# Attention and mixture of experts on one core: early attention, weight splits on VectorE alone, two elements routed at once, a layer norm ended on ScalarE

## The chip, the core and the metric

The kernel runs on one core of a Trainium2 chip. The core's engines run side by side, each working through its own instructions in order: TensorE (PE in the profile; its weight loads are PEld), VectorE (DVE), ScalarE (ACT), GpSimd (POOL) and SyncE (SP), which only issues transfers. They meet at semaphores. The metric is the time of one execution in microseconds of the device; the kernel before takes 1104.46 us (median of 3 runs, 1103.72 to 1105.25).

## What is computed

Four elements of 1024 tokens with 256 channels go through one layer of attention and a mixture of experts, in float32:

```python
# attention: 16 heads, head size 16, causal; queries, keys and values by a "down" and an "up" matrix
q_lat = (x @ Wq_down).reshape(b, t, H, L)        # the same for k and v
q = concat([q_lat @ Wq_up_c, rope(q_lat @ Wq_up_e)])
att = softmax(where(causal, q @ k.T / sqrt(DH), -inf))
x = layernorm(x + (att @ v) @ Wc)
# mixture of experts: 8 experts, 2 for each token
scores = (x @ router_w.T + router_b) / temp
for _ in range(3):                               # Sinkhorn, on each element by itself
    scores -= logsumexp(scores, over experts)
    scores -= logsumexp(scores, over the tokens of the element)
gates = exp(scores); gates /= sum(gates) + 1e-8
topk_gates, topk_idx = top 2 of gates, scaled to a sum of 1
out_e = (relu(x @ wg[e]) * (x @ wp[e])) @ wo[e]
x = layernorm(x + sum over the two experts of gate * out_e)
```

## The kernel before

Instructions are traced by Python in the order below; a planner then orders each engine's instructions by their readiness in a simulated time line and by priority, which is the order of tracing unless a block raises it. The order in which the engines run can thus differ from that of the source.

**Projection** (`project`, L234). For each element and half of 512 tokens, x is split into a high and a low part in a reduced 32-bit format, and products are made of three matmuls (`mm3`, L191: high x high, high x low, low x high). `split` (L186) makes the two parts: ScalarE casts the high one, and VectorE, or another engine given as `sub`, subtracts it from the source for the low one. Queries and keys are stored to DRAM as three bf16 parts; `load_stack` (L323) brings the parts of one group of four heads back as 12 transfers per call, all issued by SyncE.

**Attention** runs over *units* (L307): an element, a group of four heads, and its two halves of queries; for the last element (3) the first halves of two groups form a unit, and the second halves are four units of their own. For a unit, `row_max` (L341) computes scores (PE L354) and their maxima (DVE L360, and L363 with the causal mask), turns them and writes them into the stack of the queries. `attend` (L398) then computes transposed scores (PE L433), their exponentials (ACT L437, into one of three `pT` tiles), zeroes what lies above the diagonal (POOL L446; in the last two units DVE L442), and multiplies by the values (PE L417).

The main loop (L1086) attends the units one step (one head of one key block) after the other. In each step it traces as many steps of `row_max` as keep it 44 (`LEAD`) ahead, a share of the `lane` (projections of later elements and `finish` of the element before), and a share of the `side` lane (routing), whose budget is `SIDE` per attention step, or `SIDE3` for the last element. Every step of the routing costs at least 0.05 of it. Before the loop, the maxima of the whole first unit are traced, one step of the projection of element 1 with every third of them (L1067 to L1071).

**Finish** (`finish`, L541) of an element, in two halves: load x (`x1`, SP L548), turn and scale the attention's result, multiply by Wc (PE L588), add x (DVE L591), `layernorm` (L509: statistics on DVE L513 and L514, the reciprocal root on POOL L516 and L517, and the normal form on DVE L519), store it to two tables in DRAM (`x1_rows`, `results`), and compute the router's logits (L635).

**Routing** (`route`, L648) of an element: 3 iterations of the Sinkhorn loop and the choice of two experts, a chain of 73 small steps on DVE, ACT and PE; then 8 pairs of indirect transfers on GpSimd (L805) that write each token into the list of its expert. For elements before the last they are traced only in a window of eight attention steps of a unit (`hole`, set at L1133 from `HOLE`, L30). `lay_out` (L827) then works out which slots belong to which expert: first 17 slots that need the first three elements alone, then the others once element 3 is routed.

**Experts.** 35 slots of 256 tokens run one after the other (`slot`, L976, with `begin`, L1159, for the next slot in between). For a slot: load the three weights of its expert (SP L940, 1.5 MB), gather its tokens (POOL L926, two indirect transfers), split the weights (`halves`, L953: six pieces of 128x512, ACT L188 for the high parts and L189 for the low parts `wl`), turn and split the tokens (`rows`, L962), three-fold matmuls into `gp`, ReLU (ACT L992), product (DVE L993), split of the product (`hh` on ACT, `hl` on DVE, L188 and L189), three-fold matmuls into `eo`, scaling by the gate (ACT L1006, into one of `EO` = 6 tiles, two per slot), and two indirect transfers that add to `results` (POOL L1007). Each of them waits until those of the slot before have landed, as they may touch the same rows (L1014). One of the six pieces of `wl` is split on GpSimd, as `SH_A` and `SH_B` (L25) name it:

```python
split(a, c, d, nc.gpsimd if (i, k) in (SH_A if key < (0, NSA) else SH_B) else nc.vector)
```

At the end (L1187 on) the `results` are read back, normalised and stored.

## Time and profile before

| what | value |
|---|---|
| median of 3 runs | 1104.46 us |
| the profiled execution | 1105.71 us |
| its span, first to last instruction | 1104.0 us |
| mean granted clock of TensorE | 0.966 |
| busy in the span: PE, DVE, ACT, POOL | 983.1, 855.4, 708.0, 536.6 us |
| share of PE in the chain that ended last | 62% |
| opening and projection of element 0 | 0 to about 62 us |
| attention (first to last exponential) | 65.5 to about 699 us |
| expert slots (first turn of tokens to last matmul) | 701 to about 1066 us |
| last layer norm | 1078 to 1104 us |

A line of a window gives, for a stretch of time, the length, then for PE, PEld, DVE, ACT and POOL the busy time and in brackets the number of instructions, then the granted clock of TensorE, the share of the 16 DMA engines in use, and GB/s. Matmuls overlap each other, so PE's busy time can be full while it gets through fewer matmuls than it could; the number of instructions tells that. A line of the waits names the engine and its line that waited, then the engine and line that ended the wait, then the total in us, the number of waits and the longest. A line of a tile gives the shortest, the median and the longest duration in ns. A line of the timeline gives the start and the length in us, the engine, the line and the shapes, and in brackets the idle time of the engine before it and what ended that. A wait for several things is put down to the one that came last by the profile; where the named one had long been done, it was another, often a transfer.

The groups of small work that the change touches, as sums over the execution: layer norm's line L519 12.6 us on DVE in 32 instructions (mean 451 ns); the pair scatters L805 64.9 us on POOL in 64; GpSimd's splits of `wl` 61.2 us in 35 (mean 1750 ns); DVE's splits of `wl` 126.7 us in 175 and of `hl` 96.1 us in 140.

### The profile page before, as it was taken

To read this page: it belongs to the slowest core of one execution; us is meant where nothing else is said; L and a number is where in the kernel's file an instruction comes from. 1 tells how busy PE (TensorE), PEld (TensorE's weight loads), DVE (VectorE), ACT (ScalarE), POOL (GpSimd) and SP (SyncE) were. 2 spreads that over 40 slices of the span, in tenths; PEclk is the share of its full clock that TensorE was granted. 3 is DMA by queue.
4 is the path that set the end of the run, shared out by engine and by line. 5 is a ranking of instruction groups with operands and counts; after the bars stand their busy time and mean duration, and the time that the engine had idled before them with its cause. 6 is when DMAs were issued, how large, how long until landed. Compare 5 with 4: busy or idle time off the path is not lost.

```text
span 1104.0 us, 20951 instructions
## 1 busy us (share of the span) xinstructions
PE 983.1 (89%) x6808; PEld 621.3 (56%) x6808; DVE 855.4 (77%) x2516; ACT 708.0 (64%) x1701; POOL 536.6 (49%) x587
## 2 busy tenths in 40 slices
PE   6688999999999999999899999899995989999950
PEld 4445333355434355533344333599995989999950
DVE  4677777888987788887458885689993879898936
ACT  3345666656766666766666777677773767777733
POOL 7276511121534534431333405665778677777554
PEclk9899999999999999999999999999997999999985
DMA  8573410231331231421133210877763877898637
GB/s 297 177 227 94 130 44 16 59 102 59 115 106 30 74 96 37 143 73 35 26 101 102 50 39 3 271 221 216 216 187 110 235 212 201 221 230 223 179 41 304
DMA packets 92065, 146.33 MB, mean 133 GB/s; under 512 B 19760, under 2 KB 55088, under 8 KB 91568
## 3 DMA queue, kind: packets, MB, share of 16 engines
q1 hardware_dynamic: 69296, 108.50, 31.4%
q0 software_dynamic: 20608, 36.18, 14.2%
q8 instruction: 56, 0.92, 0.3%
q10 hardware_dynamic: 2048, 0.27, 0.2%
q14 instruction: 57, 0.47, 0.1%
HBM read 109.26 MB, written 35.38 MB: 131 GB/s over the span
## 4 chain that ended last, share of the span: by engine, by line
PE 62%; DVE 12%; ACT 8%; DMA 6%; issue 5%; POOL 4%; SPq 2%; ACTq 0%; DVEq 0%; POOLq 0%
PE y L417 13%; PE sT L433 9%; PE s L354 9%; ACT pT L437 4%; PE gp L197 4%; PE gp L195 4%; PE gp L196 4%; POOL pairs L805 3%; DVE wl L189 2%; PE po L588 2%; PE eo L195 2%; PE eo L196 2%; DVE d L363 2%; PE eo L197 2%; DMA results<-eo,ent 2%
## 5 line engine op out<-in xcount | busy, mean ns | idle before, releaser
L437 ACT ACTIVATE pT<-sT 128x512 f32<-128x512 f32 (+3 forms) x768 | 347.1, 491 | 176.9 <-PE sT L433 147.3
L363 DVE CUSTOM_DVE_ANT_0 d<-s,mask 128x128 bf16<-128x128 f32 (+3 forms) x512 | 236.8, 482 | 50.4 <-PE s L354 48.8
L433 PE MATMUL sT<-qs,ks 98*128 98x512 bf16 (+3 forms) x768 | 231.7, 328 | 15.8 <-ACT pT L437 11.1
L354 PE MATMUL s<-ks,qs 96*128 96x512 bf16 (+3 forms) x768 | 222.6, 331 | 21.3 <-DVE mx L363 8.0
L446 POOL TENSOR_SCALAR_AFFINE_SELECT pT<-pT 128x512 f32<-128x512 f32 x120 | 76.6, 639 | 278.3 <-ACT pT L437 262.1
L360 DVE TENSOR_REDUCE mx<-s 128x1 f32<-128x512 f32 x256 | 175.2, 684 | 31.4 <-PE s L354 30.1
L417 PE MATMUL y<-pT,va 128*32 128x512 f32 (+3 forms) x1536 | 183.2, 500 | 1.4 <-POOL pT L446 0.6
L197 PE MATMUL gp<-xh,wl 128*128 128x256 f32 x560 | 160.1, 287 | 17.3 <-POOL wl L189 15.3
L195 PE MATMUL gp<-xh,wh 128*128 128x256 f32 x560 | 160.7, 288 | 1.3 <-DVE relu L993 1.2
L196 PE MATMUL gp<-xl,wh 128*128 128x256 f32 x560 | 160.9, 288 | 0.0
L1007 POOL DMA_INDIRECT results<-eo,ent x70 | 113.9, 1628 | 80.7 <-issue 10.7
L354 PEld LDWEIGHTS <-qs 96*128 96x128 bf16 x768 | 71.6, 99 | 131.2 <-issue 96.7
L433 PEld LDWEIGHTS <-ks 98*128 98x128 bf16 x768 | 71.9, 99 | 123.4 <-issue 92.8
L189 DVE TENSOR_TENSOR wl<-w,wh 128x512 fp32r<-128x512 f32 x175 | 126.7, 758 | 15.1 <-ACT wh L188 14.2
L188 ACT CAST wh<-w 128x512 fp32r<-128x512 f32 x210 | 118.5, 622 | 4.9 <-DMA w<-in_wo_dram 1.6
L197 PEld LDWEIGHTS gp<-xh,wl 128*128 128x128 f32 x560 | 107.7, 193 | 18.6 <-POOL wl L189 16.4
L195 PEld LDWEIGHTS gp<-xh,wh 128*128 128x128 f32 x560 | 107.3, 192 | 2.6 <-DVE relu L993 2.4
L196 PEld LDWEIGHTS gp<-xl,wh 128*128 128x128 f32 x560 | 107.4, 192 | 0.1
L189 DVE TENSOR_TENSOR hl<-relu,hh 128x256 fp32r<-128x256 f32 x140 | 96.1, 692 | 14.1 <-ACT hh L188 12.2
L926 POOL DMA_INDIRECT xg<-x_rows,ent x70 | 81.2, 1160 | 29.5 <-issue 15.2
L188 ACT CAST hh<-relu 128x256 fp32r<-128x256 f32 x140 | 56.2, 406 | 49.8 <-DVE relu L993 49.3
L195 PE MATMUL eo<-wh,hh 128*128 128x256 f32 x280 | 80.4, 287 | 6.3 <-DVE xl L189 4.8
(208 smaller groups left out, 1702.2 us busy)
## 6 DMA issues: line engine op xcount, KB each, us to landing
w<-in_wg_dram SPq DMA_DIRECT2D x35, 512.0 KB, 5.7
w<-in_wp_dram SPq DMA_DIRECT2D x35, 512.0 KB, 4.9
w<-in_wo_dram SPq DMA_DIRECT2D x35, 512.0 KB, 4.4
ks<-parts SPq DMA_DIRECT2D x90, 128.0 KB, 2.8
qs<-parts SPq DMA_DIRECT2D x66, 128.0 KB, 2.7
parts<-lv POOLq DMA_DIRECT2D x12, 384.0 KB, 3.1
parts<-lv POOLq DMA_DIRECT2D x24, 192.0 KB, 3.1
xh<-in_x_t_dram SPq DMA_DIRECT2D x8, 512.0 KB, 3.8
```

Source lines behind the costliest of these rows:

```text
L188: nc.scalar.copy(hi, src)
L189: (sub or nc.vector).tensor_tensor(lo, src, hi.bitcast(F32), ALU.subtract)
L195: nc.tensor.matmul(ps, lhsT=sh, rhs=mh, start=(i == 0), stop=False)
L196: nc.tensor.matmul(ps, lhsT=sh, rhs=ml, start=False, stop=False)
L197: nc.tensor.matmul(ps, lhsT=sl, rhs=mh, start=False, stop=(i == n - 1))
L354: nc.tensor.matmul(ps[:, :w], lhsT=q(h, half)[:NROW, t * P : (t + 1) * P], rhs=k(h, k0 // QC)[:NROW, :w], start=True, stop=True,)
L360: nc.vector.tensor_reduce(m, ps, AX.X, ALU.max)
L363: nc.vector.tensor_tensor_reduce(out=dump[:, :w], in0=ps[:, :w], in1=mask[:, QC - w :], scale=1.0, scalar=MASKED, op0=ALU.add, op1=ALU.max ...
L417: nc.tensor.matmul(acc[g, qc][SLOT * h : SLOT * (h + 1), lo:], lhsT=va[b % 2][:, kb, at : at + SLOT], rhs=pT[:, h, lo:], start=(kb == 0), ...
L433: nc.tensor.matmul(st[:, lo:], lhsT=k(h, kb // BPQ)[: NROW + 2, kb % BPQ * P : (kb % BPQ + 1) * P], rhs=q(h, qc)[: NROW + 2, lo:], start=T ...
L437: nc.scalar.activation(pT[:, h, lo:], st[:, lo:], AF.Exp, scale=scale)
L1007: ins = nc.gpsimd.indirect_dma_start(out=results[:, :], out_offset=bass.IndirectOffsetOnAxis(ap=ent[:, j, 1:2], axis=0), in_=eo, in_offset ...
```

## The change

Six things change:

- **Splits.** `SH_A` and `SH_B` are empty, so all six pieces of `wl` of a slot are split on VectorE.
- **Begin of attention.** Before the main loop only 17 steps of `row_max` of the first unit are traced (its first half of queries), and five steps of the projection of element 1 instead of 16. The rest of the unit's maxima are traced inside the main loop, at most three steps for each attention step and never more than 44 ahead; the rest of the projection is in the lane.
- **Loads of x1.** The load of `x1` in `finish` is issued on SyncE's queue after the last transfer of a stack that was traced before it.
- **Routing.** Elements 0 and 1 are routed together, when element 1 is finished: tiles are twice as wide, the sums over tokens stay within an element, 16 pairs of scatters follow the 73 steps. Elements 2 and 3 are routed one by one as before. The pool of the routing's tiles has one buffer for each in place of two.
- **Share of the routing.** `SIDE` goes from 0.035 to 0.05 per attention step.
- **Layer norm in `finish`.** Two small instructions on GpSimd make an offset, minus mean times reciprocal root, and ScalarE applies scale and offset in place of VectorE.

```diff
@@ -15,14 +15,14 @@
-R_BUFS, X1_BUFS, PT_BUFS, SIDE, SCAT = (1,2,3,0.035,0.07)
+R_BUFS, X1_BUFS, PT_BUFS, SIDE, SCAT = (1,2,3,0.05,0.07)
-SH_A, SH_B, NSA = (((1,1),),((1,1),),0)
+SH_A, SH_B, NSA = ((),(),0)
@@ -88,7 +88,7 @@
-    sinkp = ctx.enter_context(tc.tile_pool(name="sinkp", bufs=2))
+    sinkp = ctx.enter_context(tc.tile_pool(name="sinkp", bufs=1))
@@ -515,9 +515,12 @@
         rstd = small.tile([P, BPQ], F32, tag="rstd", name=f"rstd_{n}", bufs=2)
         nc.gpsimd.tensor_scalar_add(rstd, mv[:, :, 1], EPS_LN)
         nc.gpsimd.tensor_tensor(rstd, rstd, neg_half, ALU.pow)
+        off = small.tile([P, BPQ], F32, tag="off", name=f"off_{n}", bufs=2)
+        nc.gpsimd.tensor_tensor(off, mv[:, :, 0], rstd, ALU.mult)
+        nc.gpsimd.tensor_scalar(off, off, -1.0, None, ALU.mult)
         for i in range(BPQ):
-            nc.vector.tensor_scalar(
-                x[:, i, :], x[:, i, :], mv[:, i, 0:1], rstd[:, i : i + 1], ALU.subtract, ALU.mult
+            nc.scalar.activation(
+                x[:, i, :], x[:, i, :], AF.Identity, bias=off[:, i : i + 1], scale=rstd[:, i : i + 1]
             )
 
     no_deps = {}
@@ -530,7 +533,9 @@
-    logits = {}
+    ROUTES = (*((b, b + 1) for b in range(0, B - 2, 2)), *((b,) for b in range((B - 2) // 2 * 2, B)))
+    logits, scores = {}, {}
@@ -540,14 +545,19 @@
 
     def finish(b, halves=range(NQC), alone=False):
         if b not in logits:
-            logits[b] = sinkp.tile([P, NB, E], F32, tag="lg", name=f"lg{b}")
+            bs = next(r for r in ROUTES if b in r)
+            lgs = sinkp.tile([P, len(bs), NB, E], F32, tag=f"lg{bs[0]}", name=f"lg{b}", bufs=1)
+            for j, of in enumerate(bs):
+                logits[of] = lgs[:, j]
+            scores[bs] = lgs
         lg = logits[b]
         for half in halves:
             n = f"{b}_{half}"
             x1 = work.tile([P, BPQ, C], F32, tag="x1", name=f"x1_{n}", bufs=X1_BUFS)
-            nc.sync.dma_start(
-                out=x1, in_=x_in[b, half * QC : (half + 1) * QC].rearrange("(n p) c -> p n c", p=P)
-            )
+            with tc.issue_after(queued[0].ins):
+                nc.sync.dma_start(
+                    out=x1, in_=x_in[b, half * QC : (half + 1) * QC].rearrange("(n p) c -> p n c", p=P)
+                )
             yns, zTs, pos, xTs, rts = {}, {}, {}, {}, {}
 
             def own_tile(name):
@@ -640,20 +650,26 @@
             yield 0.1
 
     def per_block(ap):
-        return ap.unsqueeze(2).to_broadcast([P, NB, E])
-
-    def per_expert(ap):
-        return ap.unsqueeze(1).to_broadcast([P, NB, E])
-
-    def route(b):
-
-        lg = logits[b]
+        return ap.unsqueeze(2).to_broadcast([*ap.shape, E])
+
+    def per_expert(ap, nb):
+        return ap.rearrange("p (b e) -> p b e", e=E).unsqueeze(2).to_broadcast([P, nb, NB, E])
+
+    def route(bs):
+
+        b, nb = bs[0], len(bs)
+        NBT, BE = nb * NB, nb * E
+        lgs = scores[bs]
+        lg = lgs.rearrange("p b n e -> p (b n) e")
 
         def tiny(name):
-            return sinkp.tile([P, NB], F32, tag=name, name=f"{name}{b}")
+            return sinkp.tile([P, NBT], F32, tag=name + str(nb), name=f"{name}{b}")
 
         def wide(name):
-            return sinkp.tile([P, NB, E], F32, tag=name, name=f"{name}{b}")
+            return sinkp.tile([P, NBT, E], F32, tag=name + str(nb), name=f"{name}{b}")
+
+        def by_element(ap):
+            return ap.rearrange("p (b n) e -> p b n e", b=nb)
 
         for it in range(SINKHORN_ITERS):
             m = tiny("sk_m")
@@ -673,44 +689,48 @@
             nc.vector.tensor_tensor(lg, lg, per_block(ls), ALU.subtract)
             yield 0.0
 
-            pm = sinkp.tile([P, E], F32, tag="sk_pm", name=f"sk_pm{b}_{it}")
-            nc.vector.tensor_reduce(pm, lg.rearrange("p n e -> p e n"), AX.X, ALU.max)
+            pm = sinkp.tile([P, BE], F32, tag=f"sk_pm{nb}", name=f"sk_pm{b}_{it}")
+            nc.vector.tensor_reduce(
+                pm.rearrange("p (b e) -> p b e", e=E), lgs.rearrange("p b n e -> p b e n"), AX.X, ALU.max
+            )
             yield 0.0
             tp = bg_tile(f"sk_tp{b}_{it}")
-            nc.tensor.transpose(tp[:E, :P], pm, ident)
+            nc.tensor.transpose(tp[:BE, :P], pm, ident)
             ex = wide("sk_ex")
-            nc.vector.tensor_tensor(ex, lg, per_expert(pm), ALU.subtract)
+            nc.vector.tensor_tensor(by_element(ex), lgs, per_expert(pm, nb), ALU.subtract)
             yield 0.0
             nc.scalar.activation(ex, ex, AF.Exp)
...
-            nc.tensor.matmul(tp[:, 2 * P : 2 * P + E], lhsT=ones[:E, :], rhs=dg, start=True, stop=True)
-            nc.vector.tensor_tensor(lg, lg, per_expert(tp[:, 2 * P : 2 * P + E]), ALU.subtract)
+            nc.tensor.matmul(tp[:, 2 * P : 2 * P + BE], lhsT=ones[:BE, :], rhs=dg, start=True, stop=True)
+            nc.vector.tensor_tensor(lgs, lgs, per_expert(tp[:, 2 * P : 2 * P + BE], nb), ALU.subtract)
...
-        for n in range(NB):
+        for n in range(NBT):
             while not hole[0]:
                 yield WAIT
             for k in range(2):
...
@@ -1064,9 +1084,11 @@
     drain(project(0, 1, any_tile))
     load_stack(units[0], (1,))
     load_stack(units[1])
-    first = row_max(units[0])
+    maxima = (1 if step is None else step for u in units for step in row_max(u))
     early = project(1, 0, bg_tile)
-    for n, _ in enumerate(first):
+    attended_to = maxed = 0
+    for n in range(HG * BPQ + 1):
+        maxed += next(maxima)
         if n % 3 == 2:
             next(early, None)
 
@@ -1079,9 +1101,6 @@
     sure, more = order[:SURE], order[SURE:]
     early = None
 
-
-    maxima = (1 if step is None else step for u in units[1:] for step in row_max(u))
-    attended_to, maxed = 0, HG * BPQ * sum(qc + 1 for qc in units[0][2])
     routed = [0]
     for i, unit in enumerate(units):
         b, gs, qcs = unit
@@ -1116,7 +1135,8 @@
                         load_stack(units[i + 2])
                 elif n == 4:
                     load_stack(units[i + 2])
-            while maxed < attended_to + LEAD:
+
+            while maxed < min(attended_to + LEAD, HG * BPQ + 3 * attended_to):
                 with tc.high_priority(offset=PR[0]):
                     step = next(maxima, None)
                 if step is None:
@@ -1126,7 +1146,8 @@
                 lane.give(give / steps)
             if routed[0] < b and not any(m == f"F{b - 1}" for m, _ in lane.todo):
                 routed[0] = b
-                side.add("R", route(b - 1))
+                if b - 1 in [bs[-1] for bs in ROUTES]:
+                    side.add("R", route(next(bs for bs in ROUTES if b - 1 in bs)))
                 if last:
                     side.add("T", lay_out(0))
             at = n - HG * BPQ * (len(qcs) - 1)
```

## The prediction

> **What bounds the kernel.** I read the windows first, in stretches of 10 to 150 us. From 100 to 700 us (attention) PE is busy 570.7 of 600 us, nearly all at full clock, so DVE or ScalarE time saved there buys little. The last 38 us have no matmul and are untouched. The expert slots (35 of them, 705 to 1066 us) are the place where PE loses time. One full-speed window, then the stage:
>
> ```profile
> 1000.00:1010.00 10.00, 10.00 (x87) 10.00 (x86) 8.88 (x14) 6.60 (x16) 6.49 (x6) 1.00 0.88 229
> ...
> 826.00:850.00 24.00, 10.29 (x72) 9.38 (x71) 8.04 (x18) 7.57 (x19) 19.57 (x17) 0.77 0.27 67
> 850.00:893.00 43.00, 42.93 (x354) 42.72 (x353) 36.90 (x61) 31.02 (x75) 31.25 (x24) 0.97 0.86 245
> 893.00:908.00 15.00, 11.21 (x82) 10.99 (x81) 10.88 (x19) 8.36 (x21) 11.16 (x9) 0.89 0.75 193
> 908.00:1050.00 142.00, 137.70 (x1150) 136.19 (x1149) 127.58 (x210) 105.86 (x254) 97.59 (x72) 1.00 0.82 211
> ```
>
> The count behind PE says more than its busy share. Full speed is 87 matmuls per 10 us; a slot has 48 (gp) + 24 (eo) + 4 (transposes) = 76, so 8.74 us. Against that rate the four stretches lost: 826-850, 209-72 = 137 matmuls, 15.7 us; 850-893, 20, 2.3 us; 893-908, 48, 5.6 us; 908-1050, 85, 9.8 us. Sum 33.4 us: the ceiling for the experts.
>
> Second, the waits and the tiles of the split:
>
> ```profile
> PE gp L197 <- POOL wl L189: 15.3, 2, 11.6
> ...
> L189 DVE TENSOR_TENSOR wl<-w,wh x175: 659/681/3061, 705.4 to 1056.0; 128x512 fp32r<-128x512 f32 x175
> L189 DVE TENSOR_TENSOR hl<-relu,hh x140: 401/418/2906, 717.5 to 1062.9; 128x256 fp32r<-128x256 f32 x140
> ...
> L189 POOL TENSOR_TENSOR wl<-w,wh x35: 1281/1867/1898, 707.2 to 1051.0; 128x512 fp32r<-128x512 f32 x35
> ```
>
> Two PE waits end on GpSimd's split (11.6 and 3.8 us: the holes at 835 and 899), and DVE's own splits have maxima of seven (hl) and over four (wl) times their medians. Third, why GpSimd is late: its timeline, in the burst of pair scatters and in the steady part.
>
> ```profile
> 842.79 0.96 POOL L805 DMA_INDIRECT pairs<-ent,so_i  x1 [0.30 <-issue]
> 844.06 1.60 POOL L1007 DMA_INDIRECT results<-eo,ent  x1 [0.30 <-issue]
> 845.09 1.88 POOL L189 TENSOR_TENSOR wl<-w,wh 128x512 fp32r<-128x512 f32 x1
> ...
> 909.66 1.62 POOL L1007 DMA_INDIRECT results<-eo,ent  x1 [2.21 <-ACT relu L992]
> 910.74 1.88 POOL L189 TENSOR_TENSOR wl<-w,wh 128x512 fp32r<-128x512 f32 x1
> 912.78 1.58 POOL L1007 DMA_INDIRECT results<-eo,ent  x1 [0.17 <-ACT relu L992]
> 914.66 1.26 POOL L926 DMA_INDIRECT xg<-x_rows,ent  x1 [0.30 <-issue]
> 916.23 1.21 POOL L926 DMA_INDIRECT xg<-x_rows,ent  x1 [0.30 <-issue]
> 918.34 1.62 POOL L1007 DMA_INDIRECT results<-eo,ent  x1 [0.90 <-ACT xh L188]
> ```
>
> GpSimd takes its work in order. The split at 845 stood behind 16 scatters. In the steady part each slot's first result store (L1007) may go only when the previous slot's two have landed (median 5.2, up to 6.5 us from issue), and the split sits between the slot's two stores: first to second 3.12 us, second to the next slot's first 5.56 here. From 909.66 to 1041.97 are 14 slots, 9.45 us each: GpSimd's chain of stores, split included, sets the pace, not PE's 8.74.
>
> And the hl row beside it:
>
> ```profile
> 910.03 2.88 DVE L189 TENSOR_TENSOR hl<-relu,hh 128x256 fp32r<-128x256 f32 x1
> ```
>
> It starts just before GpSimd's split and ends just after. Laid over GpSimd's rows, 33 hl and wl rows meet a split and run to 3.06 us; of the 282 that meet none, none exceeds 0.72.
>
> **The change, part by part.** Sums are against the profiled execution, 1105.7 us (span 1104.0), 1.2 above the median 1104.5.
>
> *Splits without GpSimd.* GpSimd loses 35 rows, 61.2 us. DVE gains 35 x 0.681 = 23.8 us, and loses the stretch: hl (mean 692 - median 418) x 140 = 38.4 us, wl (758 - 681) x 175 = 13.5 us, together 51.9. DVE comes out 28 us lighter. The Trainium skill, "SBUF — State Buffer", "Who interferes with whom", says that a DVE instruction with two SBUF inputs and a GpSimd instruction that reads SBUF lock each other out for a whole instruction; the rows agree in kind. By it the stretch would be at most one split per slot, 35 x 1.87 = 65 us, against the 51.9 measured.
>
> The chain of stores becomes 1.92 (first to second store where no split lies between, 891.38 to 893.31) + 6.33 (mean of the 14: (132.3 - 14 x 3.12)/14) = 8.25 us, under PE's 8.74, so PE sets the pace. 908-1050: 14 x (9.45 - 8.74) = 9.9; with landings at their 6.5 maximum the chain is about 9 and only 3 remain; I take 8. 893-908: 3.8 is the wait, 5.6 the loss; I take 5. 850-893: 0 to 2.3, I take 1.5. 826-850: the split no longer stands behind the scatters, but the stores and the gathers do. The eo ring has 6 buffers, three slots; the thirteenth slot's eo waits for the tenth's stores, which still go at 844 and land at 850. PE has that slot's gp and the next slot's meanwhile: I keep 5.7 us of the 15.7 and take 10 (4 to 15.7). Sum **-24.5** (-10 to -33.4).
>
> *First unit early.* The first 17 steps of row maxima and the projection steps among them are as before; then both kernels let attention's first half overlap the maxima of the second, since the order is by priority and readiness (sT already runs at 64.8). PE is idle 3.6 of the 20 us from 80 to 100, the most to gain; the deferred projection may cost as much later. Take **-1.5** (+2 to -3.6).
>
> *x1 loads behind the stacks.* The two loads at 4.4 us (1 MB, in 4-20 us where DMA is full at about 400 GB/s: 2.6 us) leave the opening, whose chain is the down weights ahead of them: -0.5 (0 to -2.6). Later ones go on SP's queue behind the last traced stack load. Six still arrive before use; that of element 2's second half (451.6 before) goes behind the stack issued until 569.3, lands 4.3 us later, 573.6, and its first sum stood at 568.8: 4.8 us late. Its sums, its layer norm and then routing of element 2, which ends at 670 and feeds the first slots at 701, queue behind it. Take **+1.5** net (-2.6 to +4.8).
>
> *Routing two at once.* One of four routings goes: about 15.5 us of DVE rows, 5 of PE and 5 of ScalarE, less 67 ns of width on some 45 DVE rows. PE is the one that counts: -2 (0 to -5). The cost lies in its scatters. The chain has 73 steps; begun at the second unit of element 2 at one per attention step it ends one step past the third unit's window, six of its 16 pairs go in the fourth's, and ten, 20 scatters, in one run where now 8 stand:
>
> ```profile
> 609.43 1.08 POOL L805 DMA_INDIRECT pairs<-ent,so_i  x1 [0.17 <-issue]
> ...
> 624.96 0.64 POOL L446 TENSOR_SCALAR_AFFINE_SELECT pT<-pT 128x512 f32<-128x512 f32 x1 [3.17 <-ACT pT L437]
> ```
>
> 20 x 1.27 = 25.4 us ends at 634.8; the diagonal mask due at 625 is 9.8 late, and the values matmul after it. Three pT buffers and the row maxima cover part: +3 (0 to +9.8). Single buffers in the routing's pool cost nothing: the last routing begins at 743.6, the one before it has sent its last scatter at 689.8; were that later, its waits would fall on DVE. Together **+1** (-5 to +9.8).
>
> *Layer norm on ScalarE.* 32 rows of 0.41 to 0.45 leave DVE (12.6 us busy); 32 of 0.587 (the same activation at L1222) come to ScalarE, 64% busy, 18.8 us; two GpSimd rows (0.20, 0.23) per norm. A second rule speaks against it: "Perfetto Trace Analysis", "Optimizing Scalar/DVE Operations", gives about 93 ns of access overhead for Scalar on SBUF and 60 for DVE, 32 x 33 ns = 1 us as an estimate; the rows say 4 to 6. On the path it is the wait that matters: once GpSimd's rstd came 11.3 us late (behind scatters, 680.9 to 692.2) and DVE stood still; now the exps queue behind it on ScalarE. The order is made so that norms follow their inputs, so I take **+1.5** (-1 to +11.3).
>
> Sum: -24.5 - 1.5 + 1.5 + 1 + 1.5 = -22, from 1104.5: **1082**.
>
> **Rivals.**
> (a) *The stores keep the pace.* Faster slots lengthen landings, the backlog of the burst keeps the eo ring full, so the experts give only their lower end, 10, and the +2.5 elsewhere stands: 1097. For: the chain's margin is 0.5 us per slot; against: landings of 4.5 where DMA is light.
> (b) *Everything is collected.* 31 of the 33.4 from the experts, the opening's 1.5, and nothing late elsewhere: 1072. For: PE ran full until 820 with the same stores; against: scatters still block GpSimd 23 us.
> (c) *DVE becomes the bound: slower.* If the long hl rows are not GpSimd's doing, DVE needs 127.6/(1150/76) = 8.43 + 0.68 = 9.11 us per slot; at its present share, 0.898, a slot takes 10.15 against 9.38, 35 x 0.77 = +27, less 16 of the two holes: 1104.5 + 11 + 2.5 = 1118. It decides once more than half of the stretch stays. Against it: the 33 of 33 coincidence.
> (d) *No change*: the gain is eaten by scatters in attention and waits on ScalarE, +20 in all, about 1104.
>
> **Chances.** Forecast (1076 to 1090) 0.48, (a) 0.2, (b) 0.18, (d) 0.04, (c) 0.10. The range drops most of (c) and the far end of (b): 1066 to 1098; the forecast's own is 1076 to 1090. This kernel's measurement tells 0.2% (2.2 us) from no change. Faster 0.86, same 0.04, slower 0.10.
>
> **What would show it.** hl and wl rows with maxima near 0.45 and 0.72; no split on GpSimd; first-to-second stores 1.9 us apart; a slot period of 8.7 to 8.9 with 85 to 87 matmuls per 10 us from 900 on; the hole in the scatter burst down to some 5 us; 20 scatters in a row before the diagonal masks of the first late unit of element 3. The forecast is wrong if slots stay at 9.3 or more, if DVE's busy share in the slots rises above 0.95, or if the first slot starts after 708.

## The result, and the profile after

The changed kernel is slower: 1123.35 us median of 4 runs (1118.62 to 1125.17) beside 1104.86 (1103.72 to 1111.95) for the kernel before, ratio 1.012, 95% interval [1.0082, 1.0158]; in a repetition on another chip 1.0079 [1.0040, 1.0117]. The forecast, 1082 in 1066 to 1098, is wrong in its sign. The profiled execution took 1125.17 us. Experiments ran on several chips, and every ratio below is to the kernel before on the same chip; on two of these chips that kernel itself takes 1148 to 1150 us (the last section tells what is different there).

The page of the changed kernel, parts 1 and 2 (busy time; the granted clock in 40 slices of 28 us), and below it the clock line of the kernel before:

```profile
span 1123.5 us, 20795 instructions
PE 995.5 (89%) x6794; PEld 623.0 (55%) x6794; DVE 802.3 (71%) x2451; ACT 719.2 (64%) x1717; POOL 492.3 (44%) x565
PEclk9899999999999897998989899999999899999985
```

```profile
PEclk9899999999999999999999999999997999999985
```

DVE is 53 us lighter and PE is busy 12 us longer, although it does no more work (6794 matmuls, 6808 before): the clock line has 9 everywhere through attention before, and falls to 8 and 7 here. Ends of the elements' last units, first slot and time at half clock tell where (all from chips on which the kernel before takes 1105 to 1109; us from the span's start):

| kernel | end of element 0 | 1 | 2 | 3 | first slot | half clock, 90 us to first slot |
|---|---|---|---|---|---|---|
| before | 234.6 | 403.0 | 564.1 | 704.0 | 701.1 | 3.4 |
| changed | 235.6 | 409.7 | 582.8 | 735.0 | 731.8 | 51.1 |
| changed, again | 236.3 | 408.6 | 579.5 | 729.7 | 726.5 | 34.1 |
| old opening | 236.6 | 410.0 | 574.2 | 725.4 | 722.3 | 30.7 |
| routing not merged | 232.4 | 403.9 | 572.5 | 717.8 | 716.2 | 34.1 |
| norm on DVE | 235.0 | 398.1 | 563.1 | 710.7 | 707.5 | 23.8 |
| both undone | 234.5 | 404.0 | 564.6 | 703.7 | 702.6 | 6.8 |

So 30.7 us are lost before the first slot. The slots themselves gain, though less than forecast. The "10th output" is where the `eo` matmuls of the tenth slot begin:

| kernel | first slot to 10th output | 10th to 19th | 19th to 35th | last matmul to end |
|---|---|---|---|---|
| before | 107.3 | 104.4 | 148.6 | 38.0 |
| changed | 104.0 | 97.8 | 143.1 | 42.0 |
| both undone | 110.0 | 96.2 | 141.9 | 41.4 |
| both undone, ten output buffers | 107.7 | 95.4 | 141.9 | 41.5 |
| both undone, list load held back | 108.7 | 94.3 | 143.0 | 41.6 |
| before, list load held back | 109.9 | 105.7 | 148.4 | 37.8 |

The changed kernel's row: 3.3 + 6.6 + 5.5 = 15.4 us won, 4.0 lost at the end; 30.7 - 15.4 + 4.0 = 19.3 of the 19.5 us between the spans. Windows of the changed kernel's slots, in the columns of before (the scatter burst, the hole behind it, what follows, the steady part):

```profile
855.00:881.00 26.00, 25.91 (x220) 25.71 (x219) 18.87 (x59) 16.32 (x39) 19.78 (x18) 1.00 0.28 60
881.00:896.00 15.00, 5.04 (x26) 4.84 (x25) 3.07 (x6) 3.83 (x9) 10.95 (x10) 0.69 0.65 183
896.00:915.00 19.00, 17.17 (x142) 16.97 (x142) 16.39 (x35) 15.35 (x38) 10.33 (x8) 0.97 1.06 344
915.00:1065.00 150.00, 148.41 (x1254) 147.76 (x1253) 119.36 (x248) 117.83 (x280) 93.86 (x64) 1.00 0.82 218
```

The hole has moved, not gone: PE runs on through the burst (220 matmuls in 26 us, where 72 in 24 stood), and then stands for 10 us. The tiles of the split:

```profile
L189 DVE TENSOR_TENSOR wl<-w,wh x210: 653/684/731, 736.3 to 1071.7; 128x512 fp32r<-128x512 f32 x105
L189 DVE TENSOR_TENSOR hl<-relu,hh x140: 403/417/479, 746.7 to 1078.3; 128x256 fp32r<-128x256 f32 x140
```

With GpSimd's split gone no hl row exceeds 479 ns (2906 before). The waits of the whole execution:

```profile
ACT wh L188 <- DMA w<-in_wg_dram: 14.4, 2, 12.4
PE s L354 <- DMA ks<-parts: 12.2, 5, 7.1
...
PE gp L195 <- ACT wh L188: 10.0, 1, 10.0
```

The hole now ends on ScalarE's cast, which waited 12.4 us for its weight.

### The profile page after: what moved, and what is told of

Its sections match the earlier page's. It is cut to its first block, busy times and chain, and to the rows that moved or that the text cites. A ratio compares the mean times of both kernels' runs of the same rounds, so it can differ in the third digit from the quotient of the medians.

```text
span 1123.5 us, 20795 instructions
## 1 busy us (share of the span) xinstructions
PE 995.5 (89%) x6794; PEld 623.0 (55%) x6794; DVE 802.3 (71%) x2451; ACT 719.2 (64%) x1717; POOL 492.3 (44%) x565
## 3 DMA queue, kind: packets, MB, share of 16 engines
q0 software_dynamic: 20608, 36.18, 13.7%
## 5 line engine op out<-in xcount | busy, mean ns | idle before, releaser
L433 PE MATMUL sT<-qs,ks 98*128 98x512 bf16 (+3 forms) x768 | 236.5, 336 | 21.8 <-ACT pT L437 15.0
L354 PE MATMUL s<-ks,qs 96*128 96x512 bf16 (+3 forms) x768 | 226.2, 339 | 28.6 <-DMA ks<-parts 12.2
L189 DVE TENSOR_TENSOR wl<-w,wh 128x512 fp32r<-128x512 f32 x210 | 135.6, 685 | 42.9 <-ACT wh L188 41.6
L1027 POOL DMA_INDIRECT results<-eo,ent x70 | 117.2, 1674 | 108.1 <-ACT hh L188 26.3
L195 PEld LDWEIGHTS gp<-xh,wh 128*128 128x128 f32 x560 | 106.3, 191 | 12.2 <-ACT wh L188 10.2
L946 POOL DMA_INDIRECT xg<-x_rows,ent x70 | 78.4, 1120 | 43.8 <-issue 15.8
L417 PEld LDWEIGHTS y<-pT,va 128*32 128x32 f32 x1536 | 32.9, 110 | 86.4 <-issue 46.3
L196 PE MATMUL eo<-wl,hh 128*128 128x256 f32 x280 | 78.9, 283 | 0.0
```

What stands on the lines that cost most here:

```text
L189: (sub or nc.vector).tensor_tensor(lo, src, hi.bitcast(F32), ALU.subtract)
L195: nc.tensor.matmul(ps, lhsT=sh, rhs=mh, start=(i == 0), stop=False)
L196: nc.tensor.matmul(ps, lhsT=sh, rhs=ml, start=False, stop=False)
L354: nc.tensor.matmul(ps[:, :w], lhsT=q(h, half)[:NROW, t * P : (t + 1) * P], rhs=k(h, k0 // QC)[:NROW, :w], start=True, stop=True,)
L417: nc.tensor.matmul(acc[g, qc][SLOT * h : SLOT * (h + 1), lo:], lhsT=va[b % 2][:, kb, at : at + SLOT], rhs=pT[:, h, lo:], start=(kb == 0), ...
L433: nc.tensor.matmul(st[:, lo:], lhsT=k(h, kb // BPQ)[: NROW + 2, kb % BPQ * P : (kb % BPQ + 1) * P], rhs=q(h, qc)[: NROW + 2, lo:], start=T ...
```

## The experiments

**The splits alone** (kernel before, `SH_A, SH_B = (), ()`).

> The kernel before with its weight splits on VectorE alone and nothing else changed. Theory (the experts gain about 15 us and attention, from 100 to 704 us, is left as it was; the loss of 31 us comes from the other parts): first slot's transposes at 701 as before, no new half-clock stretch before them, time 1085 to 1092. Rival (taking the splits away from GpSimd changes the planner's order of attention too, and costs there): first slot later than 712, time above 1098.

Measured: 0.9916 [0.9874, 0.9958], 1138.47 us on a chip where the kernel before takes 1150.16. The splits are worth about 0.8%. The first slot is at 745.1, yet the rival falls: up to the first expert matmul the order of instructions on every engine is that of the kernel before. The chip makes that difference; the last section shows it.

**The norm on ScalarE, and the merged routing.** Each was undone alone, and both together:

```diff
-            nc.scalar.activation(x[:, i, :], x[:, i, :], AF.Identity, bias=off[:, i : i + 1], scale=rstd[:, i : i + 1])
+            nc.vector.tensor_scalar(x[:, i, :], x[:, i, :], mv[:, i, 0:1], rstd[:, i : i + 1], ALU.subtract, ALU.mult)
...
-    ROUTES = (*((b, b + 1) for b in range(0, B - 2, 2)), *((b,) for b in range((B - 2) // 2 * 2, B)))
+    ROUTES = tuple((b,) for b in range(B))
```

> The changed kernel with the layer norm's last step back on VectorE. Theory one (the norm on ScalarE is the main cost: the exps queue behind it, and a lighter VectorE lets the row maxima run out, so that TensorE idles and its clock is halved): half-clock time in attention falls from 51 us to under 15, first slot at 705 to 712, time 1095 to 1105. Rival one (the x1 loads behind the stacks are the cost): time stays within 8 us of 1123 and the half-clock stretches stay. Rival two (the merged routing is): the same, stays.

> The changed kernel with four separate routings again (one per element, buffers and pace as before). Theory one (layer norm): within 8 us of 1123. Rival two (the merged routing, whose 20 scatters hold the diagonal masks of the last element's first late unit and which ends late): the last element's attention recovers at least 10 us of its 12 us loss, time 1108 or less.

> The changed kernel with the norm's last step back on VectorE and four separate routings: what is left of the change is the early opening, the x1 loads behind the stacks and the splits. Theory one (less VectorE work lets the instruction order put the row maxima further ahead, 87 to 89 steps instead of 73 to 78 when an element's last unit begins; two units are loaded, 96 steps, so the maxima run into the next stack's load, TensorE idles and its clock is halved): the order's lead is that of the kernel before, no wait of 1 us or more for a stack at 370 to 420, first slot within 6 us of the kernel before, time 12 to 25 us under that kernel. Rival one (the x1 loads): the loss stays, time not under the kernel before.

> The changed kernel with only the layer norm's last step back on VectorE, again, since the chip of the first batch delayed every run in its bursts of scatters. Undoing both this and the merged routing gave 18 us over the changed kernel. Theory one (the lighter VectorE is the cause, and both parts lighten it): about half of it, 1104 to 1110 beside 1116, no stack wait over 1 us at 375 and 416. Rival (the merged routing alone is the cause, by its 20 scatters): no gain, within 3 us of the changed kernel.

> The changed kernel with only the separate routings, again, for the same reason. Theory one: the stack wait at 375 stays, since the norm is still off VectorE, but nothing holds the masks of the last element's first late unit; 1104 to 1110. Rival (the norm alone is the cause): within 3 us of the changed kernel.

> The changed kernel with only the norm's last step back on VectorE, on a chip without the long stalls in scatter bursts if there is one to be had. Undoing norm and merged routing together gave 18 us over the changed kernel, 26 us of it before the first slot. From the stages that hold no scatter, the norm on ScalarE costs about 10 us between the ends of elements 0 and 1, and the merged routing gives 5.5 there: theory one says element 1 ends at 397 to 400 (404 with both undone), element 2 at 562 to 568, and the merged routing then costs in the last element by its 20 scatters, which end at 640 to 652: first slot 700 to 712, time 1095 to 1106. Rival (the merged routing carries the loss): first slot later than 718.

> The changed kernel with only the separate routings, so the norm alone moved to ScalarE. Theory one: the norm costs 10 us or so in each of the first three elements' finishes that lie in attention: element 1 ends at 410 to 416, element 2 at 575 to 588, first slot 715 to 728, time 1108 to 1120. Rival (the merged routing carries the loss): first slot before 710.

| run | undone | median us | before, same chip | ratio, 95% interval |
|---|---|---|---|---|
| after_again | nothing | 1116.55 | 1107.83 | 1.0079 [1.0040, 1.0117] |
| a_no_ln_merge | both | 1098.72 | 1107.83 | 0.9920 [0.9884, 0.9956] |
| a_no_ln3 | norm | 1100.25 | 1108.55 | 0.9931 [0.9903, 0.9958] |
| a_no_merge3 | routing | 1110.25 | 1108.55 | 1.0034 [0.9997, 1.0070] |
| a_no_ln, a_no_ln2 | norm | 1146.14, 1147.43 | 1150.16, 1147.96 | 0.9978, 0.9996 |
| a_no_merge, a_no_merge2 | routing | 1145.94, 1148.18 | 1150.16, 1147.96 | 0.9966, 1.0057 |

From the four upper rows: undoing the norm brings 1.5% (16 us), both 1.6%. Undoing the routing brings 0.45% (5 us), which two intervals of 0.4% each do not tell from nothing, and with the norm on DVE the merged routing costs 0.1%. The norm carries the loss. Of the two other chips, one doesn't separate the two parts; on the other the norm undone is 0.6% ahead, at the edge of the noise. The two parts do not simply add: with four routings the norm on ScalarE costs the stage of element 1 only 2.0 us (171.5 against 169.5; element 1 ended at 403.9, not at 410 to 416 as expected), with two routed at once 9 (172.3 against 163.1).

How it does so. 

> The changed kernel once more, as the yardstick beside the others of this batch. If the first comparison holds, 1 to 2% slower than the kernel before on the same chip, with TensorE's first two waits for a stack of keys (line 354, 1.6 us each, at 375 and 416) and half-clock stretches behind them.

Windows of the changed kernel in that run:

```profile
368.00:382.00 14.00, 11.01 (x69) 3.68 (x65) 6.03 (x24) 8.05 (x21) 2.54 (x4) 0.88 0.47 148
...
410.00:436.00 26.00, 23.36 (x130) 11.72 (x128) 11.94 (x50) 14.58 (x36) 5.85 (x10) 0.74 0.32 101
```

What TensorE waited for from 370 to 440 us in the same run:

```profile
PE s L354 <- DMA ks<-parts: 1.7, 1, 1.7
PE s L354 <- DMA qs<-nm: 1.6, 1, 1.6
```

The same windows with both undone:

```profile
368.00:382.00 14.00, 13.34 (x83) 4.42 (x81) 10.56 (x37) 9.26 (x24) 6.97 (x9) 1.00 0.40 131
...
410.00:436.00 26.00, 25.57 (x172) 13.83 (x170) 20.87 (x79) 14.62 (x34) 11.31 (x16) 1.00 0.21 72
```

130 matmuls where 172 go, and DVE half as busy: the row maxima have run out. Two units' stacks are loaded, 96 steps of maxima; the next stack's buffer comes free only when a unit's attention ends, and its loads take 8 us to issue. Counted in TensorE's instruction order, the maxima stand 74, 73, 78 and 81 steps ahead of the scores at steps 289, 313, 337 and 361 before the change, 78, 87, 89 and 87 after it, and with both undone as before. Each part moves the order: 76, 79, 80 and 82 with the norm alone undone, 82, 81, 84 and 87 with the routing alone undone. Step 337 begins a unit, and the last loaded step is then 95 ahead: 17 steps of maxima are left before the change, 6 after it. From 368.9 to 377.2 no maxima matmul runs.

The lead alone doesn't make a stall: before the change it grows to 86 by step 433, and no maxima there wait for a stack. What counts is when the first maxima of a new stack are due. For the units begun at steps 337 and 385 they run 12.9 and 13.8 us after the unit's start before the change, without a wait, and 10.4 us after it in the changed kernel, after waits of 1.7 and 1.6. TensorE's timeline at the first, in the changed kernel:

```profile
375.09 0.39 PE L433 MATMUL sT<-qs,ks 98*128 98x128 bf16 x2 [0.25 <-ACT pT L437]
377.18 0.80 PE L354 MATMUL s<-ks,qs 96*128 96x128 bf16 x3 [1.70 <-DMA ks<-parts]
...
379.97 0.63 PE L433 MATMUL sT<-qs,ks 98*128 98x512 bf16 x1
...
381.68 0.38 PE L433 MATMUL sT<-qs,ks 98*128 98x512 bf16 x1
```

The wait is 1.70 us, but the scores' matmuls after it take 0.63 instead of 0.38: half clock. By the trace's clock record it lasts from 377.2 for 3.4 us, and from 418.2 for 13.7.

**Is it the lead?** One order edge for each maxima matmul, no work added:

```diff
+    n_s, scored, CAP = [0], [], 76
...
+                        n_s[0] += 1
+                        if n_s[0] > CAP:
+                            tc.add_manual_dep(
+                                ins.ins, scored[n_s[0] - CAP - 1].ins.name,
+                                mybir.DependencyInfo(mybir.DependencyClass.NoSync, mybir.DependencyReason.SCHED_ONLY),
...
+                    scored.append(ins)
```

> The changed kernel with one thing added: a row-max matmul may stand in TensorE's order at most 76 steps ahead of the scores of the attention (an ordering edge on the same engine; no work is added). In the changed kernel the lead is 87 to 89 when units begin at steps 313 to 433; here it is 74 to 75. Theory one (maxima too far ahead run into the load of the next stack): the 1.6 us waits for a stack at 375 and 416 go, the half-clock stretches there too, element 1 ends at 401 to 405 instead of 408.6, time 8 us or more under the changed kernel. Rival (the lead does not matter; ScalarE's or GpSimd's longer queue delays the exps and masks): within 4 us of the changed kernel, half-clock stretches elsewhere instead.

Measured: 1154.82 us, 1.0056 [1.0021, 1.0091], on a chip where the kernel before takes 1147.96 and the changed one was not timed, so the total settles nothing. The stage does: from the end of element 0 to that of element 1, where the merged kernels have no scatter, it takes 167.4 us, the changed kernel 174.1 and 172.3, with the norm on DVE 163.1 in three runs, before 168.4. Its windows:

```profile
368.00:382.00 14.00, 13.37 (x89) 4.25 (x89) 10.07 (x33) 9.63 (x24) 1.91 (x3) 1.00 0.38 107
410.00:436.00 26.00, 25.55 (x177) 13.71 (x176) 19.58 (x75) 17.49 (x41) 4.30 (x8) 1.00 0.17 57
```

Both stalls and both half-clock stretches are gone, by the order alone: the first maxima of the two stacks now run 15.2 and 18.6 us after the unit's start. A stretch of 6.8 us at half clock, at 326.5 behind a wait of 1.4 us for exponentials, is new in this stage. So here the lead costs 5 to 7 us (one profile each). The 4.3 left against the norm on DVE are near ScalarE's own two norms of four rows, 8 x 0.588 = 4.7 us, but the new stretch may have its part in them. On the same chip the norm on DVE (a_no_ln2) takes 163.0, 170.9 and 180.3 us for elements 1 to 3, the capped kernel 167.4, 169.0 and 189.5: 2.5 us behind at the end of element 2, and 9 more in element 3. So the cap doesn't bring the whole loss back, and how the 16 us divide in the later elements is not settled.

**Is it DVE being light?** A twin of the norm's last step on DVE, on the mask, into scratch. The mask is 512 wide, so a row of the twin is 128x512 and takes 542 ns in the median, not the 408 of the norm's own 128x256:

```diff
+            dump = work.tile([P, QC], BF16, tag="dump", name=f"same_{n}_{i}", bufs=2)
+            nc.vector.tensor_scalar(dump, mask, mv[:, i, 0:1], rstd[:, i : i + 1], ALU.subtract, ALU.mult)
```

> The changed kernel with an idle twin of the norm's last step left on VectorE (same shape, same scalars, from the mask into a scratch tile that nothing reads), while ScalarE does the real one. It computes the same. Theory one (it is the lighter VectorE that lets the maxima run ahead): the two stack waits at 375 and 416 fall under 0.8 us and the clock stays full there; time 8 us or more under the changed kernel. Rival (it is the longer ScalarE, whose exps are late): waits and time stay within 4 us of the changed kernel.

Measured: 1148.96, 1.0377 [1.0302, 1.0451]: 32 us worse than the changed kernel. The two stack waits went, but a half-clock stretch of 13.7 us came at 242, the stage took 174.4 us, and a new collision came at 681:

```profile
DVE same L526 <- POOL rstd L517: 17.3, 1, 17.3
...
PE x1T_ps L590 <- ACT x L522: 9.9, 1, 9.9
...
PE y L417 <- POOL pT L446: 7.6, 1, 7.6
```

GpSimd's rstd and masks stood behind 16 scatters, and both engines that read rstd stood with them. In TensorE's order the maxima stand 76, 79, 80 and 82 steps ahead at the four steps above, exactly as with the norm on DVE (later they fall below that), while ScalarE still does the norm. So there it is DVE's work that sets the lead. That a lighter DVE is the cause of the whole loss the run doesn't show; work put back elsewhere gives another order with stalls of its own.

**Opening and x1 loads.** 

> The changed kernel with the old opening (all maxima of the first unit traced before any attention). Theory one: the opening is worth 0 to 4 us and the loss of attention later is untouched: within 4 us of the changed kernel. Rival (the early opening shifts the whole order and is a cause of the later loss): 8 us or more under it.

> The changed kernel with its x1 loads issued as soon as their buffer is free, as before the change. Theory one (layer norm): within 8 us of 1123. Rival one (the late x1 loads stall VectorE in front of the sums x + po, then the row maxima, then TensorE, whose clock falls): first slot at 705 to 712, half-clock time under 15 us, time 1095 to 1105.

Measured: the old opening 1113.39, 1.0067 [1.0033, 1.0102], beside 1.0079: nothing that can be told. Free x1 loads 1.0157 [1.0046, 1.0267] on a chip without a time of the changed kernel; the stage of element 1 took 173.8 us, so the loads are not what stretches it. With both attention parts undone the x1 loads stay behind the stacks, and every element ends within 1 us of the kernel before.

**The run of 20 scatters.** The merged routing at a faster pace, `SIDE` 0.07 for 0.05, norm on DVE:

> As a_no_ln3, but the merged routing runs at 0.07 instead of 0.05 of a step per attention step, so its 32 scatters go 16 and 16 in element 2 and none in the last element's first late unit. If the run of 20 scatters is what the merged routing costs: the unit that took 31 us (628 to 659 in the changed kernel, 24.3 before the change) takes 24 to 26, and the time is 4 to 10 us under a_no_ln3. Rival (the late end of element 2's routing costs, not the scatters): within 3 us of a_no_ln3.

Measured: 1109.42, 1.0011 [0.9985, 1.0037], 0.8% over a_no_ln3, where 4 to 10 us under it were expected. The unit of the 20 scatters takes 26.1 us instead of 32.3 as expected, but element 2 ends at 574.3 instead of 563.1. 16 scatters in a row at 505 us:

```profile
PE y L417 <- POOL pT L446: 11.3, 1, 11.3
```

and 20.5 us of half clock from 509.7. With 20 in a row at 607 to 631 (a_no_ln3) the same wait was 3.7 us. So a run of scatters costs wherever it stands ahead of a mask that is due; the kernel before sends eight in a window.

**The hole in the slots.** More output buffers (`EO` 10 for 6), both attention parts undone:

> Both attention parts undone (norm on VectorE, four routings) and ten buffers for the scaled outputs instead of six. With six, TensorE stands 8.9 us at 852 for a buffer whose store waits behind the last 16 scatters on GpSimd, and its clock is halved for 10.2 us after. If the ring of output buffers makes this hole: two more slots of matmuls fit before it, the hole shrinks to under 3 us and the time falls 5 to 12 us under the run with six, 1086 to 1094. If the hole comes from the second list of rows, which the same scatters hold up: hole and time stay within 3 us.

> Both attention parts undone and ten output buffers, again, beside the others. With six buffers the hole was 8.9 us at 852 with 10.2 us of half clock behind it; with ten, on a chip that stalled in scatters, no hole over 3 us. Expected here: no hole over 3 us in the burst, 4 to 8 us under the run with six, a ratio of 0.984 to 0.990 to the kernel before.

Measured: 0.9898 [0.9819, 0.9977] and 0.9927 [0.9899, 0.9956], the latter beside 0.9920 with six: no gain, and the hole stays at 8.52 us. The longest wait of SP's queue in that run:

```profile
SPq L934 <- DMA pairs<-ent,so_i: 32.0, 2, 16.0
```

The timeline around it, SP's issues and ScalarE's row behind them:

```profile
834.72 0.37 SPq L957 DMA_DIRECT2D w<-in_wo_dram  x1
854.05 0.34 SPq L934 DMA_DIRECT2D ent<-pairs  x1
854.90 0.37 SPq L957 DMA_DIRECT2D w<-in_wg_dram  x1
...
859.69 0.62 ACT L188 CAST wh<-w 128x512 fp32r<-128x512 f32 x1 [10.79 <-DMA w<-in_wg_dram]
```

The load of the first pairs of the second list waits for the last scatters, 16 us. The weight loads stand behind it in SP's queue, ScalarE's cast waits for them, its casts of hh stand behind that cast, and PE waits for hh. In the changed kernel the same load waits 15.3 us. So this load was put behind the weights of the two slots before it, alone:

```diff
-        for i, (step, depth) in enumerate(((pairs_of, EA), (weights, W_BUFS), (gather, GA))):
+        steps = ((0, pairs_of, EA), (1, weights, W_BUFS), (2, gather, GA))
+        for i, step, depth in (steps[1], steps[0], steps[2]) if n == NA - 2 else steps:
             while counts[i] < min(n + depth, len(keys)):
+                if not i and counts[0] >= NA and n < NA - 2:
+                    break
```

> Norm on VectorE, four routings, six output buffers, and the first list load of the second row list goes onto SP's queue two slots later, behind the weights of slots 15 and 16. Ten output buffers left the hole at 852 (8.5 us), so the ring is not its cause. Theory: SP's queue is; the pair load (line 934) waits 16 us for the last scatters, weight loads stand behind it, ScalarE's cast waits 11 us for them with the casts of hh behind it. Then the hole falls under 3 us, no half clock follows, and the time is 8 to 13 us under the run with six buffers and the old place: 1085 to 1091 on a chip without scatter stalls, ratio 0.980 to 0.985. Rival (the second list's rows are gathered behind the same scatters, and PE runs out of slots anyway): the hole moves to the transposes of slot 17, 5 us or more, and at most 4 us are won.

> The kernel before, with only the list load held back in the same way. If the hole of 11.6 us at 835 in that kernel came from GpSimd's weight split behind the scatters, as the forecast said, it stays within 3 us and so does the time (ratio 0.997 to 1.003). If it came from SP's queue there too: the hole falls under 5 us and the time by 6 us or more.

Measured: with both parts undone 0.9919 [0.9886, 0.9951], no gain in time where 8 to 13 us were expected. The hole of 8.9 us is now two, 3.39 at 852.7 and 4.12 at 860.6, and what ends them has changed once more:

```profile
ACT eo L1026 <- DMA results<-eo,ent: 11.8, 2, 6.2
...
PE eo L195 <- ACT eo L1026: 4.6, 2, 4.1
```

Now it is the output ring, its stores behind the scatters. On the kernel before the same edit gives 1.0059 [1.0023, 1.0094], some 5 us more that no trace here explains, and the hole stays at 11.55 us:

```profile
PE gp L197 <- POOL wl L189: 11.6, 1, 11.6
```

There GpSimd's split ends it, as the forecast had it. Three waits lie on top of each other behind these 16 scatters: the split, SP's queue, the ring. Held-back load and ten buffers were not run together.

Faster than both kernels are the changed one without the norm and the merged routing, 0.9920, and without the norm alone, 0.9931. The splits alone give 0.9916 on their chip, so what the best of these runs wins is what the splits win.

## Why the prediction was wrong

Before the first slot the forecast had +2.5 us and the result has +30.7; for the slots and the end it had -24.5, and the result has -11.4.

*The step that failed* is the reading under "What bounds the kernel": PE busy 570.7 of 600 us in attention, "nearly all at full clock, so DVE or ScalarE time saved there buys little". That saving wasn't free. It changes the order of TensorE's instructions: of the maxima whose stacks are loaded, 17 steps are left at a unit's start (step 337) before and 6 after, PE stands and its clock falls. In the stage of element 1 this is shown by the order alone, 5 to 7 us; in the later elements the cause of the loss stays open beyond the part that carries it, the norm. The forecast's rivals had no case in which PE's clock falls.

*Layer norm on ScalarE*, +1.5 (-1 to +11.3): 16 us. The rows are as priced (588 ns, 32 of them), and the wait that was feared, for GpSimd's offset, is 1.2 us in all:

```profile
L522 ACT ACTIVATE x<-x,off,rstd x32: 584/588/602, 240.0 to 755.7; 128x256 f32<-128x256 f32 x32
...
  POOL off L520: 1.2, 2
```

The 12.6 us taken off DVE were entered as a saving; the maxima they let ahead were not followed.

*Routing two at once*, +1 (-5 to +9.8): 5 us with the norm on ScalarE and 1 with it on DVE, neither clear of the noise. The mechanism was right: 20 scatters in one run, ending at 651 in the repetition, the unit 31.3 us instead of 24.3; the gain of one routing less is element 1's, 163.1 against 169.5 us, more than the 2 (0 to 5) that were entered for it.

*x1 loads* (+1.5) and *first unit early* (-1.5): nothing that these runs can tell, within the ranges.

*Splits without GpSimd*, -24.5: right in mechanism, but twice what came. The experts and the end give 15.4 - 4.0 = 11.4 in the changed kernel, 8.8 with both undone. Three terms were mis-sized. The full rate: with both undone PE is busy all 132 us from 908 to 1040 with 1121 matmuls, 84.9 for each 10 us, not the 87 read from one window; at 84.9 the ceiling of 33.4 becomes 28.7, and a slot takes 8.95 us, not 8.74 (measured 143.1/16 = 8.94). The burst: 10 of 15.7 us were to come and the ring to keep the rest; SP's queue, which the forecast did not look at for this step, takes the hole first. The end, "untouched": from the last matmul to the start of the last store are 10.0 us instead of 6.3. From the burst on GpSimd's stores stand 16 to 19 us behind their outputs (8 to 9 before), and 9.9 against 6.2 at the last slot. PE is busy 148.4 of 150 us all the same, so the forecast's rival (a) comes true at the end alone. With only the routing undone the stores stand 7 to 14 us behind, and the end takes 34.1 us; what sets the backlog is not settled.

Of its signs, hl and wl maxima of 0.48 and 0.73 us, stores 1.9 us apart and DVE busy 119.4 of 150 us hold. Two do not: a slot takes 8.94 us with 83.6 matmuls for each 10 us, and the hole is 10 us, not some 5. The one it named for its failure holds too: the first slot after 708.

*Rival (c)*, slower through DVE, did not happen; the kernel got slower by another way.

## What to carry to other kernels

Time taken off an engine that is not the bottleneck still changes the order in which the bottleneck is fed: find what the freed engine lets run ahead, how far the buffers let it, and what stands when they end. Where a hole is removed, ask at once which wait ends next in the same place; here three lay one on the other behind the same scatters, on three queues. Read a full rate from a long stretch in which the engine is busy throughout, not from the best 10 us.

## What the runs showed of the hardware

**The clock can halve without a long wait.** In the repetition, in the 3.4 us ahead of the stretches at 377.2 and 418.2, PE was busy 1.30 and 1.82 us, with no single wait over 1.7:

```profile
373.80:377.20 3.40, 1.30 (x13) 0.43 (x6) 0.00 (x0) 1.67 (x6) 0.63 (x1) 1.00 0.63 181
414.80:418.20 3.40, 1.82 (x17) 1.29 (x16) 1.23 (x7) 2.27 (x8) 2.28 (x3) 1.00 0.83 271
```

In the profiled execution of the result the clock fell at 374.7 for 10.2 us, before the wait for the stack (375.0 to 376.7) and behind 3.4 us in which no wait was over 0.36:

```profile
371.30:374.70 3.40, 2.20 (x15) 0.68 (x14) 0.28 (x1) 2.10 (x7) 0.66 (x2) 1.00 0.41 123
```

So there the wait isn't what halves the clock; it and the thin stretch ahead of it come from the same order, in which PE has no maxima left to run between the steps of attention (none from 368.9 to 376.7). All stretches of half clock between 90 us and the first slot last 3.4 us or a multiple. At half clock that is 1.7 to 7 us more for stretches of 3.4 to 13.7, an estimate from their lengths. The Trainium skill, "TensorE: Matmul & The Clock Gate", section "What's actually happening", gives a free-running window of 3413 ns, which agrees. Its section "Why this matters for your kernels" advises against idle gaps over some 3 us; here the clock fell after gaps of 0.36 to 1.7 us.

No limit comes out of these traces. With the old opening the clock stayed full behind 3.4 us with PE busy 1.52 (from 689.6) and fell behind 3.4 us with PE busy 3.00 (from 324.4); with only the routing undone a wait of 2.0 us at 373 was followed by no half clock. Why the stretch at 418.2 lasts four times 3.4 us, with PE busy in all of it, stays open too.

**On some chips everything stands during a burst of scatters.** The run of the splits alone executes attention in exactly the order of the kernel before. The same burst of eight, a window of each, the kernel before first:

```profile
614.00:619.00 5.00, 4.63 (x30) 1.75 (x31) 4.38 (x16) 4.41 (x12) 3.78 (x5) 1.00 0.62 108
```

```profile
633.00:638.00 5.00, 0.06 (x1) 0.00 (x0) 0.36 (x3) 0.60 (x1) 3.78 (x5) 0.87 0.58 106
```

ScalarE's timeline in that window, the splits alone:

```profile
637.30 0.60 ACT L437 ACTIVATE pT<-sT 128x512 f32<-128x512 f32 x1 [5.47 <-remote]
```

GpSimd's scatters keep their pace (3.78 us busy in both), while PE, DVE and ScalarE wait, for something that the profile can't name ("remote"). Element ends differ by 2.2 us until 322 us and by 42 at the end, and grow in the bursts alone. These profiles also lack many semaphore events, 16,426 recorded against 19,129, so whether the chip or its recorder is held up stays open.
